# A two-layer graph network: the first layer's vector, tensor and scalar work in hand-set stages, in the order of the source

## The chip, the cores and the metric

The kernel runs on one core of a Trainium2 chip. The metric is the device time of one execution in microseconds; the time before is the median of 11 runs, 1776.19 us (1766.92 to 1780.38).

## The reference

There are 6,250 nodes with 128 features and about 106,000 directed edges (50,000 pairs, both ways, and a loop for each node), sorted by destination. Two layers follow each other, each on a normalized and rectified copy of the node features, and each added to them:

```python
h = jnp.maximum(_layernorm(x), 0.0)
xw = h @ W
out = segment_sum(xw[src] * (dinv[src] * dinv[dst])[:, None], dst) + b   # over the edges and a loop
x = x + relu(out)                                                      # first layer
h = jnp.maximum(_layernorm(x), 0.0)
q, k, v = h[src] @ Wq.T + bq, h[dst] @ Wk.T + bk, h[dst] @ Wv.T + bv   # 8 heads of 16
e = exp(clip(sum(q * k, head) / 4, -10, 10))
out = segment_sum(e / segment_sum(e, src)[src] * v, src) + h
x = x + layernorm(out) * gamma + beta                                  # second layer
```

`dinv` is one over the root of a node's degree. The first layer sums over edges by destination, the second by source, so the kernel also sorts the edges by source while it works on the first layer.

## The kernel before

Nodes are held in 49 blocks of 128; edges, sorted by destination, in 831 tiles of 128, four tiles to a group. A head computes degrees and the table `gtab` of scaled `xw` rows. Then `layer0` runs, and `layer1` after a branch on a flag that `layer0` works out. The change is in `layer0` alone.

`layer0` does three things beside each other.

- **Gathered blocks.** Blocks 16 to 48 are summed by gathering rows. The loop over 142 groups (`GA` to `NG0`) issues four gathers on GpSimd's queue (line 398; five buffers `gt` of four tiles), four matmuls of the gathered rows with a one-hot of the destination into PSUM (`ps`, line 957), and an add of the sum into `acc` at an offset read from memory (`add`, line 939). The one-hot is made three groups ahead (line 928).
- **Counted blocks.** The first 16 blocks (`PC`) need no gather. Windows of edges are fetched (`fetch_windows`, 4 fetches on GpSimd's queue), `count_pair` makes one-hots (`win_oh`, line 772) and `put_counts` multiplies them into counts of edges between nodes (`cb`, line 783, copied by ScalarE into the one tile `counts`, line 786); `product` multiplies a block's counts with the table in three bfloat16 parts, 147 matmuls (line 798).
- **Sorting.** `keys`, 50 sign passes on ScalarE (`counts`, line 537), 25 `rank`s on VectorE (a compare, a scan, a predicated copy, lines 553 to 556), `positions`, then `place` for each of the 831 tiles: one-hots on VectorE (`oh_tau`, line 646; lane tiles `ol`, lines 625 and 627, for eight tiles at a time), a scaled copy on ScalarE (`ola`, line 644), and `put`, six tiles later, matmuls into `pp` (line 659).

A finished block goes through `finish0`, a generator whose parts are run one at a time by `advance`: the own row's add, bias and rectifier, statistics, a normalized copy `hs`, a transpose, the projection to q, k, v (lines 893 and 894), and the split of q (and of k, v for the first 18 blocks) into three bfloat16 parts. Each part ends in writes on SP's queue. PSUM for these chains comes from two banks (`bank`, `let_go`, `free`).

`beside(k)` runs pieces of two lists, `todo` (sorting) and `more` (counted blocks), up to a share that grows with the step k; each piece has a cost that is a weight and no time. In this version these functions only record instructions. The order on each engine is set by the framework's planner, which puts together what it expects to be ready; the source's order is a priority for it. So the source's steps and the order on the chip differ.

Of the kernel before, what the change touches and what calls it, by code (L numbers as in the profile page):

```python
# [19 lines left out]
PE = mybir.EngineType.PE  # L20

P = 128
# [18 lines left out]
CQ = 4  # L41
CR = 8
# [11 lines left out]
class Kernel:  # L54
# [347 lines left out]
    def layer0(self):  # L402
# [19 lines left out]
        with ExitStack() as l0c:  # L422
# [199 lines left out]

            def lanes(t0, n):
                r["ol"] = l0.tile([P, 2, P, PT], F16, name="ol", bufs=2)
                nc.vector.tensor_tensor(r["ol"][:, 0, :, :n], self.lanes[:, :, :n],  # L625
                                        r["lane"][:, None, t0:t0 + n].to_broadcast([P, P, n]), op=OP.is_equal)
                nc.vector.tensor_tensor(r["ol"][:, 1, :, :n], r["ol"][:, 0, :, :n],  # L627
                                        r["b"][:, None, t0:t0 + n].to_broadcast([P, P, n]), op=OP.mult)

            def place(t):  # L630
                lo, hi = window(t)
                on_vector = t // PT % 4 == 3
                if t % PT == 0:
                    n = min(PT, EC - t)
                    lanes(t, n)
                    if on_vector:
                        r["ola"] = l0.tile([P, P, PT], F16, name="ola_v", bufs=1)
                        nc.vector.tensor_tensor(r["ola"][:, :, :n], r["ol"][:, 0, :, :n],
                                                r["a16"][:, None, t:t + n].to_broadcast([P, P, n]), op=OP.mult)
                if on_vector:  # L640
                    ola = r["ola"][:, :, t % PT]
                else:
                    ola = l0.tile([P, P], F16, name="ola", bufs=LAG + 4)
                    nc.scalar.activation(ola, r["ol"][:, 0, :, t % PT], AF.Copy, scale=r["a"][:, t:t + 1])  # L644
                oh = l0.tile([P, CELLS_IN * NB], F16, name="oh_tau", bufs=LAG + 4)
                nc.vector.tensor_scalar(oh[:, :(hi + 1 - lo) * NB], self.slot16[:, lo * NB:(hi + 1) * NB],  # L646
                                        r["code"][:, t:t + 1], None, op0=OP.is_equal)
                placed.append((t, lo, hi, oh, r["ol"], ola))
                if len(placed) > LAG:
                    put()  # L650
# [81 lines left out]
            def fetch_windows(q):  # L732
                rows = l0.tile([P, 2, P], I32, name="win", bufs=2)
                m = CQ * CW
                nc.gpsimd.indirect_dma_start(
                    out=rows[:m].rearrange("p a b -> p (a b)"), out_offset=None, in_=self.wins,
                    in_offset=bass.IndirectOffsetOnAxis(ap=self.win_row[:m, q:q + 1], axis=0))
                ints = l0.tile([P, 2, P], I32, name="win_int", bufs=1)
                nc.vector.tensor_scalar(ints[:m, 0, :], rows[:m, 0, :], 7, None, op0=OP.arith_shift_right)
                nc.vector.tensor_scalar(ints[:m, 1, :], rows[:m, 0, :], P - 1, None, op0=OP.bitwise_and)  # L740

                val = l0.tile([P, 2, P], F32, name="win_val", bufs=1)
                nc.vector.tensor_scalar(val[:m, 0, :], rows[:m, 1, :], self.win_node[:m, q:q + 1], float(NB),
                                        op0=OP.subtract, op1=OP.mult)
                nc.vector.tensor_tensor(val[:m, 0, :], val[:m, 0, :], ints[:m, 0, :], op=OP.add)
                nc.vector.tensor_copy(val[:m, 1, :], ints[:m, 1, :])
                pt, k = bank()
                for i in range(2):
                    nc.tensor.transpose(pt[:, i * P:i * P + m], val[:m, i, :], self.ident[:m, :m])
                code = l0.tile([P, P], F32, name="win_code", bufs=2)  # L750
                nc.scalar.copy(code[:, :m], pt[:, :m])
                lane = l0.tile([P, P], F16, name="win_lane", bufs=2)
                nc.scalar.copy(lane[:, :m], pt[:, P:P + m])
                let_go(k)
                wins[q] = [code, lane]

            counted = []

            def count_pair(b, j):
# [3 lines left out]
                oh = l0.tile([P, 2, 256], F16, name="win_oh", bufs=4)  # L763
# [12 lines left out]
                if len(counted) > 2:  # L776
                    put_counts()

            def put_counts():
                j, oh, ols = counted.pop(0)  # L780
                cb = cbps.tile([P, 512], F32, name="cb")
                for h in range(2):
                    nc.tensor.matmul(cb[:, h * CN * NB:(h + 1) * CN * NB], ols[h], oh[:, h, :CN * NB], start=True,  # L783
                                     stop=True)
# [3 lines left out]
            prods, done = {}, {}  # L788

            def product(b, b0, b1):  # L790
                if b0 == 0:
                    while counted:
                        put_counts()
# [6 lines left out]
                if b1 == NB:  # L800
                    done[b] = prods.pop(b)
                    chains.append(finish0(b, done[b]))
# [3 lines left out]
            todo += [(2, lambda b=b, n=n: counts(b, n), 0) for b, n in groups(NB + 1, 5)] + [(1, offsets, 1)]  # L806
# [9 lines left out]
            more = []  # L816
            for b in range(PC):
                if b % CQ == 0:
                    more.append((0.1 if b else 1.0, lambda q=b // CQ: fetch_windows(q), 1))
                more += [(0.6, lambda b=b, j=j: count_pair(b, j), 0) for j in range(CW // 2)]  # L820
                more += [(1.0, lambda b=b, k=k, n=n: product(b, k, k + n), 0) for k, n in groups(NB, 17)]
# [6 lines left out]
                     [more, lambda k: n2 * (k - 4) / (half - 4), 0.0]]  # L828
            chains = []

            def beside(k):
                for l in lists:
                    while l[0] and l[2] < l[1](k):
                        c, f, wants = l[0][0]
                        if wants and not free() or l[0] is more and done:
                            break
# [3 lines left out]

            def advance():
                for c in chains[:]:
                    if next(c, 0) == 0:
                        chains.remove(c)
# [16 lines left out]
            def finish0(b, po=None):  # L861
                own, xs = loads.pop(b)
                if po is None:
# [5 lines left out]
                    while not free():  # L869
                        yield 1  # L870
                    po, k = bank()
                    nc.tensor.transpose(po[:, :P], mine, self.ident)
                    nc.vector.tensor_add(own, own, po[:, :P])
                    let_go(k)
                else:
                    nc.vector.tensor_add(own, own, po[:, :P])
                    done.pop(b)
                nc.vector.scalar_tensor_tensor(own, own, self.dinv[:, b:b + 1], self.b0_r, op0=OP.mult, op1=OP.add)
                nc.vector.scalar_tensor_tensor(xs[:, 0, :], own, 0.0, xs[:, 0, :], op0=OP.max, op1=OP.add)
                rs, nm = self.stats(fin, xs, 1, self.eps0)  # L880
# [3 lines left out]
                nc.sync.dma_start(xtab_v[:, b, :], xs[:, 0, :])  # L884
                yield 1
                while not free():
                    yield 1
# [9 lines left out]
                kv = qkv[:, D:]  # L897
                nc.sync.dma_start(kvtab_v[:, b, :], kv)
                nc.sync.dma_start(owntab_v[:, b, :], qkv[:, :D])

                qp = fin.tile([P, 3, D], BF16, name="qp")
                q = fin.tile([P, D], F32, name="q")
                nc.scalar.copy(qp[:, 0, :], pw[:, P:2 * P])
                nc.vector.tensor_sub(q, pw[:, P:2 * P], qp[:, 0, :])
                let_go(k)
                if b < PB:
                    kvp = fin.tile([P, 3, 2 * D], BF16, name="kvp", bufs=1)
                    nc.scalar.copy(kvp[:, 0, :], kv)
                    r1 = fin.tile([P, 2 * D], F32, name="r1", bufs=1)
                    nc.vector.tensor_sub(r1, kv, kvp[:, 0, :])  # L910
                yield 1
                nc.scalar.copy(qp[:, 1, :], q)
                if b < PB:
                    nc.scalar.copy(kvp[:, 1, :], r1)
                nc.vector.tensor_sub(qp[:, 2, :], q, qp[:, 1, :])
# [7 lines left out]
            ohs, sums, ats = {}, {}, {}  # L923
# [7 lines left out]
            def add(g):  # L931
# [8 lines left out]
                while blocks and self.done_at[blocks[0]] <= g:  # L940
                    chains.append(finish0(blocks.pop(0)))

            load0(blocks[0])
            for g in range(GA, GA + 3):
                onehot(g)
            for g in range(GA, self.NG0):
                n = size[g]
                gt = self.rows_of_l0.tile([P, G0, D], F32, name="gt")
                for j in range(n):
                    self.gather(gt[:, j, :], self.gtab, idx0, g * G0 + j)  # L950
                if g + 3 < self.NG0:
                    onehot(g + 3)
                beside(g - GA + 1)
                oh = ohs.pop(g)
                ps = sums[g] = l0ps.tile([P, WIN], F32, name="ps")
                for j in range(n):
                    nc.tensor.matmul(ps, gt[:, j, :], oh[:, j, :], start=(j == 0), stop=(j == n - 1))  # L957
                if g > GA:
                    add(g - 1)
                advance()  # L960
            add(self.NG0 - 1)
            while chains:
                advance()
# [641 lines left out]
```

## Time and profile before

| | |
|---|---|
| median of 11 runs | 1776.19 us |
| profiled execution | 1771.92 us |
| its span | 1769.8 us |
| TensorE matmuls busy | 1495.3 us (84%) |
| VectorE busy | 1500.7 us (85%) |
| ScalarE busy | 968.6 us (55%) |
| GpSimd busy | 1169.7 us (66%) |
| mean granted TensorE clock | 0.877 |
| first gather of the first layer | 72.1 us |
| last gather of the first layer | 951.5 us |
| layer 1's first matmul | 996.0 us |

The profile is of one execution; times within it count from the start of its span. "Busy" is the union of an engine's instructions. A matmul's end is modelled, so a busy TensorE need not be at its peak. Register loads and semaphore instructions are not counted as busy. An arrow in a wait names what ended it.

### The profile page before, as it was taken

Reading aid. Unit: us, or ns where it says so; the run is one execution under the profiler, and the core shown is the slowest. Engines: PE = TensorE matmul, PEld = TensorE weight load, DVE = VectorE, ACT = ScalarE, POOL = GpSimd, SP = SyncE. Lnnn points to the kernel's source line nnn. Section 1 sums busy time; section 2 is a strip of 40 time slices with the busy share of each in tenths; the row PEclk is TensorE's granted clock in tenths of the full one; section 3 lists DMA queues with packets and bytes.
Section 4 is the critical chain, followed back from the end, with each engine's and each line's share of the span. In section 5 each row is a group of like instructions: output and inputs, shape, how many; then the busy total and the mean of one; then the engine's idle time right before and its main releaser. Section 6 shows DMA issues by size and latency. Waiting matters only on the chain. (4 is left out here: it accounts for less than half of the span.)

```text
span 1769.8 us, 41293 instructions
## 1 busy us (share of the span) xinstructions
PE 1495.3 (84%) x14772; PEld 1319.9 (75%) x14772; DVE 1500.7 (85%) x4532; ACT 968.6 (55%) x2507; POOL 1169.7 (66%) x1124
## 2 busy tenths in 40 slices
PE   3356788888878889988875499999999999999997
PEld 2346676777667767765663489999999999999997
DVE  8852399998987989999982598998998998998988
ACT  6745544444437788888751244544544544544545
POOL 0377762467567777777774777777677677677660
PEclk9756699999978555699985799999999999999999
DMA  5412232333223222222234975575565655565540
GB/s 118 112 48 58 76 106 78 85 99 101 80 81 104 70 72 73 68 70 67 73 80 151 296 223 176 161 240 174 175 211 170 197 174 175 173 187 157 171 146 25
DMA packets 168378, 225.46 MB, mean 127 GB/s; under 512 B 30187, under 2 KB 127964, under 8 KB 168164
## 3 DMA queue, kind: packets, MB, share of 16 engines
q0 software_dynamic: 45264, 112.89, 23.1%
q1 hardware_dynamic: 116551, 106.65, 19.7%
q10 hardware_dynamic: 6348, 3.20, 0.8%
q8 instruction: 118, 1.93, 0.5%
q14 instruction: 97, 0.79, 0.1%
HBM read 191.42 MB, written 31.20 MB: 126 GB/s over the span
## 5 line engine op out<-in xcount | busy, mean ns | idle before, releaser
L398 POOL DMA_INDIRECT gt<-gtab,idx x567 | 608.8, 1074 | 334.8 <-issue 138.7
L398 POOL DMA_INDIRECT kv<-kvtab,idx x539 | 550.9, 1022 | 193.0 <-issue 125.7
L1041 PE MATMUL pk<-kvp,ohD 128*128 128x256 bf16 x2646 | 314.1, 273 | 5.3 <-ACT kvn L1044 5.3
L644 ACT ACTIVATE ola<-ol,a_f 128x128 f16<-128x128 f16 x624 | 270.4, 524 | 39.0 <-DVE ol L625 35.7
L1041 PEld LDWEIGHTS <-ohD 128*128 128x128 bf16 x2646 | 258.9, 98 | 35.4 <-issue 5.9
L957 PE MATMUL ps<-oh,gt 128*128 128x64 f32 x1134 | 215.7, 334 | 78.0 <-DMA gt<-gtab,idx 31.4
L957 PEld LDWEIGHTS ps<-oh,gt 128*128 128x128 f32 x1134 | 193.4, 246 | 97.0 <-DMA gt<-gtab,idx 36.7
L1049 PE MATMUL pq<-qb,ohT 128*128 128x128 bf16 x2940 | 205.6, 219 | 0.0
L659 PE MATMUL pp<-oh_tau,ol 128*128 128x49 f16 (+5 forms) x916 | 182.5, 258 | 15.4 <-DVE ol L627 12.9
L1067 ACT ACTIVATE ex<-att 128x32 f32<-128x32 f32 x245 | 56.3, 230 | 254.5 <-DVE att L1065 246.3
L1049 PEld LDWEIGHTS <-ohT 128*128 128x128 bf16 x2940 | 185.7, 98 | 5.2
L646 DVE TENSOR_SCALAR oh_tau<-slot,code 128x98 f16<-128x98 f16 (+5 forms) x831 | 172.0, 273 | 3.4 <-PE pp L659 3.4
L786 ACT CAST counts<-cb 128x490 bf16<-128x490 f32 x208 | 112.8, 575 | 108.5 <-PE cb L783 107.6
L798 PEld LDWEIGHTS <-counts 128*128 128x128 bf16 x2352 | 166.3, 153 | 6.9 <-ACT counts L786 6.1
L798 PE MATMUL cb<-xwp,counts 128*128 128x128 bf16 x2352 | 167.1, 239 | 4.1 <-ACT counts L786 4.1
L1063 DVE TENSOR_REDUCE att<-pr 128x32 f32<-128x512 f32 x245 | 165.0, 674 | 0.6
L1055 ACT COPY oh<-ot 128x512 f32<-128x512 f32 x245 | 141.5, 578 | 43.1 <-PE ot L1053 43.0
L659 PE MATMUL pp<-oh_tau,ola 128*128 128x49 f16 (+5 forms) x688 | 143.8, 252 | 19.2 <-ACT ola L644 2.3
L659 PEld LDWEIGHTS <-ol 128*128 128x128 f16 x916 | 128.9, 154 | 25.9 <-DVE ol L627 20.4
L1044 ACT COPY kvn<-pk 128x512 f32<-128x512 f32 x196 | 110.3, 576 | 38.5 <-PE pk L1041 38.0
L659 PEld LDWEIGHTS <-ola 128*128 128x128 f16 x688 | 72.7, 114 | 74.1 <-ACT ola L644 68.5
L783 PE MATMUL cb<-win_oh,win_ol 128*128 128x245 f16 x416 | 86.0, 298 | 48.6 <-DVE win_oh L772 21.7
(1282 smaller groups left out, 2841.4 us busy)
## 6 DMA issues: line engine op xcount, KB each, us to landing
lr<-lrow SPq DMA_DIRECT2D x48, 640.0 KB
dr<-drow SPq DMA_DIRECT2D x48, 288.0 KB
gt<-gtab,idx POOLq DMA_INDIRECT x567
kv<-kvtab,idx POOLq DMA_INDIRECT x539
kvtab<-kvout SPq DMA_DIRECT2D x49, 128.0 KB
kvo<-kvtab SPq DMA_DIRECT2D x5, 1024.0 KB
qtab<-qp SPq DMA_DIRECT2D x49, 96.0 KB
qb<-qtab SPq DMA_DIRECT2D x48, 96.0 KB
```

Source lines behind the costliest of these rows:

```text
L398: self.nc.gpsimd.indirect_dma_start(out=to, out_offset=None, in_=table, in_offset=bass.IndirectOffsetOnAxis(ap=idx[:, t:t + 1], axis=0))
L644: nc.scalar.activation(ola, r["ol"][:, 0, :, t % PT], AF.Copy, scale=r["a"][:, t:t + 1])
L646: nc.vector.tensor_scalar(oh[:, :(hi + 1 - lo) * NB], self.slot16[:, lo * NB:(hi + 1) * NB], r["code"][:, t:t + 1], None, op0=OP.is_equal)
L659: nc.tensor.matmul(pp[:, h, (x0 - f0) * NB:(x1 - f0) * NB], o, oh[:, (x0 - lo) * NB:(x1 - lo) * NB], start=False, stop=t == EC - 1, skip_g ...
L786: nc.scalar.copy(self.counts[:, c0:c0 + 2 * CN, :].rearrange("p n b -> p (n b)"), cb[:, :2 * CN * NB])
L798: nc.tensor.matmul(prods[b][:, :D], self.counts[:, :P, k], self.xwp[:, k, x, :], start=(k, x) == (0, 0), stop=(k, x) == (NB - 1, 2))
L957: nc.tensor.matmul(ps, gt[:, j, :], oh[:, j, :], start=(j == 0), stop=(j == n - 1))
L1041: nc.tensor.matmul(pk[:, i - c, :], ohD[:, h, i * P:(i + 1) * P], kvp[:, 2 * tiles[i] + h, x, :], start=(h, x) == mine[0], stop=(h, x) == ...
L1044: nc.scalar.copy(kv[:, c:c + w, :], pk[:, :w, :])
L1049: nc.tensor.matmul(pq[:, i * D:(i + 1) * D], left, qb[:, x * D:(x + 1) * D], start=(x == 0), stop=(x == 2))
L1055: nc.scalar.copy(oh[:, :n, :], ot[:, :n, :])
L1063: nc.vector.tensor_reduce(att[:, :n * H], pr[:, :n, :].rearrange("p g (h d) -> p (g h) d", h=H), axis=AX.X, op=OP.add)
```

## The change

VectorE, TensorE and ScalarE keep the source's order inside the loop (`tc.manual_schedule`), and the source is set out in stages to suit that. GpSimd's and SP's queues are still ordered by the planner.

- In step g the loop now issues the gathers of group g, then the matmuls of group g - 2, the add of g - 3, the one-hot of g itself, the own-row adds of finished products (`take_products`), one part of each chain (`advance`), and the lists (`beside`).
- `fetch_windows` is split into asking, turning and keeping; the asking is some pairs ahead. A pair's one-hots are multiplied four pairs later (`CP`), not two, and a block's product stands after the first four pairs of the next block, in pieces of 9 and not 17.
- `beside` takes pieces of both lists in turn, and a list that must wait no longer ends the other's turn. `more` starts at step 1 and not 4; the weights change, and sign passes are single pieces.
- Chains keep two stages apart, and `finish0` has more and shorter stages; the split of q reads the copy in SBUF; the write of `xtab` is issued ahead of the statistics.
- The one-hots of pairs and of placing share one set of nine buffers, `wide`, where pairs had four and placing ten.

On each engine the instructions are nearly the same in number and size; their order is not. In the new order the first product (step 6), the first rank (step 26), the position step (61), the first placed tile (67) and the last (129) can be read off the built program.

```diff
+CP = 4
...
+            WIDE = LAG + 3
...
-                oh = l0.tile([P, CELLS_IN * NB], F16, name="oh_tau", bufs=LAG + 4)
+                oh = l0.tile([P, 2, 256], F16, name="wide", bufs=WIDE).rearrange("p a b -> p (a b)")
...
-                oh = l0.tile([P, 2, 256], F16, name="win_oh", bufs=4)
+                oh = l0.tile([P, 2, 256], F16, name="wide", bufs=WIDE)
...
-                if len(counted) > 2:
+                if len(counted) > CP:
...
+            def take_products():
+                while due:
+                    b = due.pop(0)
+                    own = loads[b][0]
+                    nc.vector.tensor_add(own, own, done.pop(b)[:, :P])
+                    chains.append([0, finish0(b)])
...
-            todo += [(2, lambda b=b, n=n: counts(b, n), 0) for b, n in groups(NB + 1, 5)] + [(1, offsets, 1)]
+            todo += [(1.2, lambda b=b: counts(b, 1), 0) for b in range(NB + 1)] + [(1, offsets, 1)]
...
+            def products(b):
+                return [(0.5, lambda k=k, n=n: product(b, k, k + n), 0) for k, n in groups(NB, 9)]
...
             for b in range(PC):
...
+                these = pairs(b)
+                if b:
+                    these[CP:CP] = products(b - 1)
...
+            more += [(0.2, put_counts, 0)] * CP + products(PC - 1)
...
-                     [more, lambda k: n2 * (k - 4) / (half - 4), 0.0]]
+                     [more, lambda k: n2 * (k - 1) / (half - 1), 0.0]]
...
             def advance():
+                before = 99
                 for c in chains[:]:
-                    if next(c, 0) == 0:
-                        chains.remove(c)
+                    if c[0] + 2 <= before:
+                        moved = next(c[1], 0)
+                        if moved == 0:
+                            chains.remove(c)
+                            continue
+                        c[0] += moved == 1
+                    before = c[0]
...
-            for g in range(GA, GA + 3):
-                onehot(g)
-            for g in range(GA, self.NG0):
-                n = size[g]
-                gt = self.rows_of_l0.tile([P, G0, D], F32, name="gt")
-                for j in range(n):
-                    self.gather(gt[:, j, :], self.gtab, idx0, g * G0 + j)
-                if g + 3 < self.NG0:
-                    onehot(g + 3)
-                beside(g - GA + 1)
-                oh = ohs.pop(g)
-                ps = sums[g] = l0ps.tile([P, WIN], F32, name="ps")
-                for j in range(n):
-                    nc.tensor.matmul(ps, gt[:, j, :], oh[:, j, :], start=(j == 0), stop=(j == n - 1))
-                if g > GA:
-                    add(g - 1)
-                advance()
-            add(self.NG0 - 1)
-            while chains:
-                advance()
+            with tc.manual_schedule(engines={DVE, PE, ACT}):
+                for g in range(GA, self.NG0 + 3):
+                    if g < self.NG0:
+                        gt = gts[g] = self.rows_of_l0.tile([P, G0, D], F32, name="gt")
+                        for j in range(size[g]):
+                            self.gather(gt[:, j, :], self.gtab, idx0, g * G0 + j)
+                    if GA <= g - 2 < self.NG0:
+                        gt, oh, n = gts.pop(g - 2), ohs.pop(g - 2), size[g - 2]
+                        ps = sums[g - 2] = l0ps.tile([P, WIN], F32, name="ps")
+                        for j in range(n):
+                            nc.tensor.matmul(ps, gt[:, j, :], oh[:, j, :], start=(j == 0), stop=(j == n - 1))
+                    if GA <= g - 3:
+                        add(g - 3)
+                    if g < self.NG0:
+                        onehot(g)
+                    take_products()
+                    advance()
+                    beside(g - GA + 1)
+                while chains or todo:
+                    advance()
+                    beside(2 * steps)
```

## The prediction

> **What bounds the kernel now.** I read the busy rows in 40 slices (44.2 us each) first, for where no engine is full.
>
> ```profile
> PE   3356788888878889988875499999999999999997
> DVE  8852399998987989999982598998998998998988
> POOL 0377762467567777777774777777677677677660
> PEclk9756699999978555699985799999999999999999
> ```
>
> Layer 1 starts in the 23rd slice and is not touched by the change, so it ends as much earlier or later as the first layer does. Inside the first layer VectorE (DVE) has a hole in slices 4 and 5 (digits 2, 3) and is full later; GpSimd (POOL), which issues the gathers, has its holes where VectorE is full. Engines that take turns in being late are what to look for. So I cut the first layer into stages, first all engines, then POOL's gathers alone (line 398; "x" is their number):
>
> ```profile
> 107.00:225.00 118.00, 82.35 (x549) 67.80 (x550) 42.60 (x176) 65.03 (x137) 89.97 (x93) 0.62 0.25 66
> 225.00:541.00 316.00, 259.20 (x2719) 227.54 (x2719) 287.80 (x891) 144.48 (x370) 175.24 (x164) 0.91 0.32 89
> 560.00:907.00 347.00, 303.42 (x2323) 230.23 (x2324) 329.17 (x1293) 280.48 (x690) 270.27 (x245) 0.77 0.27 72
> ```
>
> ```profile
> 107.00:225.00 118.00, 86.99 (x90) 0.62 0.25 66
> 225.00:541.00 316.00, 175.24 (x164) 0.91 0.32 89
> 560.00:907.00 347.00, 270.27 (x245) 0.77 0.27 72
> 907.00:952.00 45.00, 34.34 (x36) 0.62 0.31 79
> ```
>
> Columns: PE, weight loads, VectorE, ScalarE, POOL, clock, DMA. Until 225 us the gathers run at 118/90 = 1.31 us each, VectorE is 36% busy. From 225 to 541 VectorE is 91% busy and a gather takes 1.93 us. From 560 to 907 (the placing of edge tiles) VectorE is 95% busy and a gather takes 1.42 us. Who holds the gathers in the middle stage is in the waits (us, times, longest), here from 250 to 550 us; the last line is of 550 to 900:
>
> ```profile
> POOL gt L398 <- PE ps L957: 67.2, 9, 20.9
> POOL gt L398 <- PE cb L783: 19.4, 11, 10.3
> ```
>
> ```profile
> POOL gt L398 <- PE pp L659: 14.9, 46, 0.8
> ```
>
> A gather waits up to 20.9 us for the matmul that frees its buffer. Why the middle stage is so full stands in the timeline:
>
> ```profile
> 158.10 11.66 PE L798 MATMUL cb<-xwp,counts 128*128 128x128 bf16 x147
> 206.61 11.38 PE L798 MATMUL cb<-xwp,counts 128*128 128x128 bf16 x147 [0.72 <-ACT counts L786]
> 218.03 0.29 DVE L876 TENSOR_TENSOR own<-own,cb 128x128 f32<-128x128 f32 x1 [8.03 <-PE cb L798]
> 225.04 2.07 DVE L555 TENSOR_TENSOR_SCAN scan<-keep,init,pp 128x896 f32<-128x896 f16 x1
> ```
>
> By 225 us only two of the 16 block products are done, and the first of 25 rank scans starts there. The other 14 products and all ranks are packed into the next 316 us. In the chain that ended last the last gather starts at 951.47 and layer 1's first matmul at 996: those 45 us of drain and loads stay.
>
> ```profile
> 951.47 3.63 DMA gt<-gtab,idx
> 960.63 9.93 DMA htab<-hs
> 989.96 5.92 DMA qb<-qtab
> ```
>
> **The change, part by part.** The profiled execution took 1771.92 us (span 1769.8); the median of the runs is 4.3 us above it. I work out the start of the last gather, 951.5 before, and put the difference on the median. Steps are counted as in the new loop, one step for each of the 142 groups of four gathers. What an instruction occupies is taken start to start from runs of the same kind in the trace.
>
> *Until step 25.* The fetch of the windows stands behind 20 gathers on POOL's queue, as before, so the first window values come at 108 us in both. Three of the four fetches now stand together there; the third needs the first one's buffer, which VectorE reads at 108: 1 us at most. From step 2 on the new order makes a product about every four steps: five are done by step 25. VectorE has 79 us of work in steps 2 to 25, which is no bound. POOL alone would allow step 25 (it needs 88 gathers) at 108 + 68 x 1.31 = 197, about 200 us. TensorE decides: in four steps one product (147 matmuls at 134.49/1911 = 0.070, or 23.03/294 = 0.078 in the slow clock: 10.3 to 11.5 us), 26 matmuls of count pairs (0.12 at full clock, 0.20 in the mean of 225 to 541: 3.1 to 5.2), four groups of gather matmuls (45.60 us for 318 rows of eight a group: 1.15; in the slow clock 1.97: 4.6 to 7.9), a chain's transposes and projection (1.5). That is 19.5 to 26.1 us, 4.9 to 6.5 a step. I take 5.1, near the fast end, because the long product itself is where the clock rose in the trace. Step 25 then stands at 108 + 23 x 5.1 = 225 us; bounds 200 and 258. So the first rank comes when it came before, but with five products behind it and not two.
>
> The Trainium skill (TensorE: Matmul & The Clock Gate, "What's actually happening") says the half clock is the default and one busy window of about 3.4 us lifts it. By its half clock for everything the four steps would take 26 us, my slow bound; the trace agrees that it lifts inside a product, and that from 107 to 225 the mean grant was 0.62.
>
> *Steps 26 to 61*, the ranks, are VectorE's: 25 ranks of 0.95 + 1.99 + 1.11 = 4.05 us (101), 230 one-hots of 0.205 (47), 29 lane tiles of 0.61 (18), 36 times a group's one-hot and add, 0.34 + 0.13 (17), 18 chains of 1.6 (29), the position step (18), five reads of the accumulator offsets (1.7 each, 8), two window turns (3): 241 us. In the old middle stage VectorE, those reads included, was filled to about 94%. With a fixed order I take 93%: 259 us; bounds 97% and 88%, 248 and 274. TensorE's 4.9 a step is below VectorE's 6.7. Here POOL falls behind VectorE's pace and waits on its five buffers; that costs nothing more.
>
> *Steps 62 to 66* have 12 us of VectorE work but the last two products on TensorE, waited for by the own-row add at the next step: 2 x 10.5 + 5 x 1.15 + 1.5 = 28 us (25 to 31).
>
> *Placing*, steps 67 to 129. The same instructions in nearly the same order as before: 803 tiles took 347 us with their chains and groups, 0.432 each; 831 make 359. The one-hots now share nine buffers and not ten; a little more, 362. Bounds 350 (the 351 us of VectorE work without a gap) and 385.
>
> *The end.* Old placing ended at 907 with 36 gathers to go in 44 us. At step 130 POOL can be four groups ahead, 32 gathers at 1.25: 40 us. Chains now keep two stages apart, which costs two or three stages of about 1.5 us after the last gather: 4 us (0 to 8).
>
> Sum: 225 + 259 + 28 + 362 + 40 = 914, with 4 for the end 918, against 951.5: 33.5 us less. 1776.2 - 33.5 = 1743. With all bounds at their good ends 200 + 248 + 25 + 350 + 40 = 863 (-88); at their bad ends 258 + 274 + 31 + 385 + 44 + 8 = 1000 (+48). Not all meet; my own range for this case is -65 to -5.
>
> Things with one answer: the read of q from SBUF where PSUM was read, the table write moved ahead of the statistics, the written-out statistics: same engines, same sizes, nothing on the path. Earlier release of a PSUM bank helps a chain that is now staged anyway. SP's transfers keep the planner's order: a write that waits holds up loads for later blocks behind it. Before, one write held SP for 86.4 us, and VectorE's own-row adds waited for TensorE alone (35.6 us), never for their load; I cost it at nothing, and at one load's few us a chain if that cover goes.
>
> One more price is POOL's own. Where VectorE is idle an issue takes 0.97 us (98 to 225 us), where it is 95% busy 1.11. If the whole layer ran at the 1.42 us spacing of placing, 547 gathers after 108 us would end at 885: below my 914, so it is no bound yet, but little below. The Trainium skill (SBUF — State Buffer, "A bandwidth-pool intuition" and the box ahead of it on DMAs issued by GpSimd) speaks against filling VectorE: its two-port modes lock GpSimd out while it writes descriptors. By its example (620 ns alone, about 3100 beside VectorE, a factor of five) 547 gathers would take an estimated 2,800 us; the trace shows 14% on the issue.
>
> **The rivals.** *Gathers become the bound early* (faster still): step 25 at 200 us and ranks at 97%: 25 + 11 us on top of the forecast, -70, 1707. For it: the 67.2 us wait goes away. Against: TensorE's 0.62 clock in that stage.
>
> *Placing loses its slack* (slower). TensorE, in fixed order, now does a group's four matmuls in one piece (1.04 to 1.97 us) and a chain's projection (1.59 + 0.53 in the slow clock) ahead of the tiles; VectorE's one-hots can be six tiles ahead in a queue of nine, so three tiles, 1.3 us, are all that hides it. Before, the group's matmuls stood two by two between tiles, and VectorE waited only 6 us here for TensorE. The price is 0.2 us a step if only steps with a projection show it, 1.4 if each does; 0.9 over 63 steps is 57 us: 914 turns into 971, 1776 + 23 = 1799. It decides from 33.5/63 = 0.53 us a step.
>
> *TensorE stays at the half clock* through the first stage and VectorE waits for products: 258 and 274 in the sum, 48 us more than forecast: 966 against 951.5, 1791. For it: the 0.62 of that stage. Against: 0.91 in the next, where TensorE is 82% busy, as it would be here. Where two thirds of it hold, there is no difference.
>
> **How the numbers follow.** Forecast 0.50, gathers early 0.20, placing 0.20, half clock 0.10. A measurement of this kernel tells 0.2%, 3.6 us, from no change. Faster: 0.50 (less 0.02) + 0.20 + 0.03 = 0.71; same 0.04; slower 0.25. The range leaves out the lowest third of the second case and the upper half of the slower ones: 1703 to 1792; the likeliest case alone is 1711 to 1771.
>
> **What would show it.** Right: VectorE's digits in slices 4 and 5 rise to 5 or more; five products before the first scan; no gather waits over 10 us; the first scan near 225 us, first placed tile near 512, last gather near 914. Wrong: step 25 later than 258 us, or a placing stage over 385 us with VectorE waiting for TensorE on the shared one-hot buffers, or layer 1 longer than its 774 us.

## The result, and the profile after

The changed kernel takes **1884.51 us** (median of 8 runs, 1880.44 to 1887.24), where before takes 1775.84 (31 runs): a ratio of 1.0613, interval 1.0597 to 1.0629. It is 108.7 us slower, where 33 us less were forecast. The profiled execution took 1883.37 us, its span 1880.8. Layer 1 takes 772.9 us (773.4 before), so all of it lies in the first layer: its last gather starts at 1062.4 us and not at 951.5.

The busy rows of the changed kernel, a slice being 47.0 us:

```profile
PE   4367678776875788888887649999999999999997
DVE  8753349877866689999998349899899998998988
POOL 0365355545553567777767477777767767677670
PEclk9666778677676655678998569999999999999999
```

VectorE's hole in slices 4 and 5 is still there (3, 3; 5 or more was forecast), and a second one has opened in slices 12 to 14 (6, 6, 6). The granted clock, at 9 in slices 6 to 11 before, is 6 to 8 there now. The same stages, cut where first rank and placing now begin (columns as before: PE, weight loads, VectorE, ScalarE, POOL, clock, DMA), and then POOL's gathers alone:

```profile
107.00:290.00 183.00, 137.36 (x1145) 119.52 (x1145) 81.83 (x333) 108.30 (x239) 94.98 (x96) 0.69 0.23 64
290.00:571.00 281.00, 208.79 (x1882) 181.79 (x1880) 223.46 (x578) 95.71 (x234) 149.62 (x138) 0.73 0.26 73
635.00:1012.00 377.00, 313.88 (x2398) 244.83 (x2397) 356.23 (x1348) 297.30 (x726) 271.79 (x252) 0.74 0.26 70
```

```profile
107.00:290.00 183.00, 93.78 (x94) 0.69 0.23 64
...
1012.00:1062.00 50.00, 37.09 (x39) 0.62 0.33 88
```

Until the first rank a gather now takes 183/94 = 1.95 us, not 1.31. In the middle stage VectorE is busy 80% (223 of 281), not 91%, and the clock is 0.73, not 0.91. Only placing is as full as it was (356 of 377, 94%). The gathers' waits, of 285 to 640 us and then of 635 to 1012:

```profile
POOL gt L400 <- PE ps L1008: 78.2, 15, 12.0
...
POOL gt L400 <- PE cb L796: 16.5, 10, 4.1
```

```profile
POOL gt L400 <- PE pp L664: 27.6, 38, 3.8
```

The waits for the matmul that frees a buffer have not gone: the longest is 12.0 us where it was 20.9, but there are 15 of them where there were 9. What stands there now is in the timeline: two products, the add that takes the second, and the first rank's scan.

```profile
153.52 10.96 PE L809 MATMUL cb<-xwp,counts 128*128 128x128 bf16 x147
...
184.11 11.02 PE L809 MATMUL cb<-xwp,counts 128*128 128x128 bf16 x147
...
195.16 0.29 DVE L821 TENSOR_TENSOR own<-own,cb 128x128 f32<-128x128 f32 x1 [11.96 <-PE cb L809]
...
290.33 2.08 DVE L557 TENSOR_TENSOR_SCAN scan<-keep,init,pp 128x896 f32<-128x896 f16 x1
```

VectorE stands still for 11.96 us, the whole of the product, with nothing that may pass the add. The chain that ended last has kept its tail (1107.9 - 1062.4 = 45.5 us from the last gather to layer 1, 45 before):

```profile
1062.36 3.38 DMA gt<-gtab,idx
...
1071.14 9.74 DMA qtab<-qp
...
1101.04 6.41 DMA qb<-qtab
```

### The profile page after: what moved, and what is told of

Same layout as the page of the kernel before. It is cut to its first block, busy times and chain, and to the rows that moved or that the text cites. A ratio compares the mean times of both kernels' runs of the same rounds, so it can differ in the third digit from the quotient of the medians.

```text
span 1880.8 us, 41151 instructions
## 1 busy us (share of the span) xinstructions
PE 1534.0 (82%) x14772; PEld 1360.0 (72%) x14772; DVE 1532.9 (82%) x4532; ACT 977.8 (52%) x2507; POOL 1163.3 (62%) x1124
## 5 line engine op out<-in xcount | busy, mean ns | idle before, releaser
L1008 PE MATMUL ps<-oh,gt 128*128 128x64 f32 x1134 | 210.4, 347 | 11.4 <-DMA gt<-gtab,idx 6.3
L1008 PEld LDWEIGHTS ps<-oh,gt 128*128 128x128 f32 x1134 | 201.4, 265 | 14.5 <-DMA gt<-gtab,idx 7.8
L664 PE MATMUL pp<-wide,ol 128*128 128x49 f16 (+5 forms) x916 | 183.4, 261 | 34.3 <-DVE wide L651 33.8
L809 PEld LDWEIGHTS <-counts 128*128 128x128 bf16 x2352 | 178.3, 154 | 21.1 <-ACT counts L799 18.6
L809 PE MATMUL cb<-xwp,counts 128*128 128x128 bf16 x2352 | 179.8, 248 | 13.7 <-ACT counts L799 13.7
L796 PE MATMUL cb<-wide,win_ol 128*128 128x245 f16 x416 | 97.6, 356 | 102.0 <-ACT counts L799 63.3
L664 PE MATMUL pp<-wide,ola 128*128 128x49 f16 (+5 forms) x688 | 147.4, 258 | 28.9 <-ACT ola L649 12.4
L651 DVE TENSOR_SCALAR wide<-slot,code 128x98 f16<-128x98 f16 (+5 forms) x831 | 160.6, 277 | 5.1 <-PE pp L664 4.9
L796 PEld LDWEIGHTS <-win_ol 128*128 128x128 f16 x416 | 59.3, 159 | 129.5 <-issue 82.4
```

Source lines behind the costliest of these rows:

```text
L664: nc.tensor.matmul(pp[:, h, (x0 - f0) * NB:(x1 - f0) * NB], o, oh[:, (x0 - lo) * NB:(x1 - lo) * NB], start=False, stop=t == EC - 1, skip_g ...
L809: nc.tensor.matmul(prods[b][:, :D], self.counts[:, :P, k], self.xwp[:, k, x, :], start=(k, x) == (0, 0), stop=(k, x) == (NB - 1, 2))
```

## The experiments

The change has two halves: the new stages, and the order held on three engines. Theory A says that the held order costs the time, theory B the stages. Further theories say which engine and by what; they are named as they came up; A1, A2 and A3 put the cost on ScalarE, TensorE and VectorE.

e1 to e8, e13 to e16 and e18 ran on chips where every kernel is slower: before takes 2216 to 2270 us there, layer 1 some 1060 to 1110. Those runs are compared only by their ratio to before on the same chip and among themselves. e9 to e12 and e17 ran on chips like that of the first measurement (before at 1772 to 1776).

### Which held order costs the time

All of these are the changed kernel with another set of engines in one line; e1, e6 and e10 hold none.

```diff
-            with tc.manual_schedule(engines={DVE, PE, ACT}):
+            if True:                                          # e1, e6, e10
+            with tc.manual_schedule(engines={DVE, PE}):       # e2, e16, e18
+            with tc.manual_schedule(engines={DVE, ACT}):      # e3, e15
+            with tc.manual_schedule(engines={PE, ACT}):       # e4, e11
+            with tc.manual_schedule(engines={PE}):            # e13, e17
+            with tc.manual_schedule(engines={ACT}):           # e14
```

**e1 to e4.**

> The changed source with its stages, but no engine held to the source's order: the planner orders all five. Theory A (the loss comes from holding engines to the source's order): the product and the count pairs overlap again, the stage up to the first rank scan shortens from 290 to about 230 us, and the time falls to 1750 to 1800. Theory B (the stages themselves, lags of two and three groups and products cut in and put between pairs, cost it): about 1884 as in the changed kernel, at least 1850.

> VectorE and TensorE held to the source's order, ScalarE not. Theory A1 (ScalarE's fixed order is the cause: a sign pass of 1.2 us stands between every two count copies, so TensorE waits for its PSUM buffer): a pair takes 0.6 and not 1.5 us, five products come 8 us a product earlier, first scan at about 240 us and not 290, time 1830 to 1845. Theory A2 (TensorE's fixed order is: a product of 11 to 14 us in one piece, with VectorE's next step waiting for it): no change, 1875 to 1890.

> VectorE and ScalarE held, TensorE not. Theory A2: VectorE's waits for products (78 us) and for gather matmuls (78 us) go mostly, time below 1820. Theory A1: only the part that is not ScalarE's, time 1860 to 1885.

> TensorE and ScalarE held, VectorE not. VectorE can then go past a wait for a product to the one-hots of later pairs and to ranks. Theory A3 (VectorE's fixed order is the cause, as it alone stands still for 12 us at an own-row add): time below 1820. Theories A1 and A2: 1860 to 1885, since a free VectorE runs ahead only as far as the nine one-hot buffers let it.

Measured, as ratios to before (2270.48): e1 0.989 (0.985 to 0.993), e2 0.998 (0.993 to 1.003), e3 1.013 (1.004 to 1.022), e4 0.989 (0.984 to 0.993). The numbers expected belong to the other chips, and none of the four was as slow as 1.06. So the changed kernel itself was needed as a yardstick.

**A yardstick (e5, e6).**

> The changed kernel itself, as the yardstick for the others on the same chip. All theories: about 1884 us where the kernel before takes 1776 (ratio 1.06), first layer's last gather near 1062, signs done near 283, step 25 near 286.

> The new stages, but no engine held to the source's order (on a chip where e5 is the yardstick). Theory A (the held order costs it): 1750 to 1790 us, 95 to 130 less than e5. Theory B (the stages and their order of recording cost it, the planner cannot mend that): 1850 to 1885. Theory P (a count pair waits on TensorE for a copy that stands behind a sign pass on ScalarE, which a planner may reorder): 1790 to 1830, signs done before 260.

e5, the changed kernel: 2294.97 us, ratio 1.012 (1.005 to 1.019), not 1.06. e6: 2249.51, 0.993 (0.988 to 0.998). On these chips the held order costs 45 us, and most of the loss is not there. In their profile TensorE has idle time that nothing in the profile explains ("issue"), and the mean granted clock is lower in layer 1 too (0.88 from 1200 to 1900 us of e5, 1.00 from 1120 to 1820 of the changed kernel's first profile). Here are waits of e5 in layer 1 (1200 to 1900 us), which the change does not touch:

```profile
PEld L1096 <- issue: 88.0, 117, 2.1
...
PE pk L1096 <- issue: 57.2, 101, 2.3
```

In the first profile of the changed kernel matmuls have no such wait there, and the weight loads of that line 5.9 us over the whole run. What makes it was not found.

**e9 to e11.**

> The kernel before, unchanged, profiled on the chip of this call. It tells two readings of the runs so far apart, in which layer 1 took about 1105 us and not 773 on the chips of two calls. If the chip's slowness stretches every stage alike, the first layer of before takes 879 x 1.08 = 950 us there (the changed kernel's went from 990 to 1067), and its middle stage about 340. If it stretches above all the stages in which the engines are full, the first layer takes 1020 to 1060. On a chip where layer 1 takes 773 all agree: 1776, first layer 879.

> The new stages, no engine held to the source's order, as in e1 and e6. Where layer 1 takes 773 us: theory A (the held order costs the 108 us) 1760 to 1790; theory B (the stages cost it) 1860 to 1890. If the loss of 29 us and the gain of 45 measured on the other chips scale with nothing, 1830 to 1845, half and half. Where layer 1 takes 1105 us: ratio 0.99 as before.

> The changed kernel with VectorE alone free of the held order, TensorE and ScalarE held. Theory A3 (VectorE stands at adds for TensorE's products and gather matmuls, with other work behind them): nearly all of e10's gain over the changed kernel, within 15 us of e10. Theory A2 (TensorE's held order: count pairs wait there for ScalarE's copies) or A1 (ScalarE's): at most a third of e10's gain.

e9 took 1770.76 us with a first layer (first to last gather) of 877.6: the chip is like the first ones, and e9's question of the slower chips stays open. e10, the stages with no engine held, takes **1726.29 us**, ratio 0.973 (0.962 to 0.983), 46 us less than before (1772.02) and 158 less than the changed kernel, which was measured on another chip; by the two ratios it is 157. Theory B falls; theory A holds with a larger sum than it was given. e10 is the fastest version of this study. e11, VectorE free and the other two held, takes 1835.05, 1.034 (1.022 to 1.046): 49 us, a third of the 158, come with VectorE's order on top of the other two. That is what A1 and A2 said and far from A3.

**e13 to e18.**

> TensorE alone held to the source's order. Numbers for a chip on which before takes 1772 to 1776, none held 1726, TensorE and ScalarE held 1835, all three 1884. Theory T (TensorE's held order is the price): 1800 to 1835. Theory S (ScalarE's held order is): 1726 to 1750. Theory TS (only the two together, since a free ScalarE would copy counts in time): 1726 to 1760, and e14 as low.

> ScalarE alone held. Theory T: 1726 to 1745. Theory S: 1790 to 1835, with the sign passes done near 283 as in the changed kernel and not near 206 as with none held. Theory TS: 1726 to 1760.

> VectorE and ScalarE held, TensorE free. Theory T: 1740 to 1785, TensorE's free order takes away most of 158 us. Theory S: 1850 to 1885. Theory TS: 1750 to 1800. VectorE's own share, 49 us by e11, would remain in the first and last case: 1775.

> VectorE and TensorE held, ScalarE free. Theory T: 1850 to 1885. Theory S: 1740 to 1785, signs done near 206. Theory TS: 1775 to 1800.

> TensorE alone held, again, for a chip where before takes 1772 to 1776. Theory S (ScalarE's held order is the price, as e13 and e14 say of their chip): 1705 to 1745, as fast as none held (1726) or faster. Theory T (TensorE's): 1800 to 1835, clock in the first stage near 0.7 as in e11. In between, 1745 to 1800, both share it. On a chip like e13's: ratio 0.98 to 0.99.

> The changed kernel with ScalarE alone free of the held order (VectorE and TensorE held, as in e2 and e16), for a chip where before takes 1772 to 1776. If each engine has its own price: 1758 + 49 = 1807, signs done near 206. If ScalarE's price needs TensorE held (count pairs) but VectorE's needs ScalarE held: 1758 to 1775. If VectorE's order alone would already make TensorE wait as ScalarE's does: 1850 to 1885. On a chip like e2's: ratio 0.99 to 1.01.

Ratios to before, all sets together:

| held | slower chips | chips as at first |
|---|---|---|
| none | 0.989 (e1), 0.993 (e6) | 0.973 (e10), 1726 us |
| TensorE | 0.983 (0.972 to 0.994) (e13) | 0.990 (0.986 to 0.994) (e17), 1758 us |
| ScalarE | 1.025 (1.014 to 1.037) (e14) | not run |
| TensorE, ScalarE | 0.989 (e4) | 1.034 (e11), 1835 us |
| VectorE, ScalarE | 1.013 (e3), 1.020 (1.007 to 1.033) (e15) | not run |
| VectorE, TensorE | 0.998 (e2), 1.005 (1.000 to 1.009) (e18) | not run |
| all three | 1.012 (e5) | 1.061, 1884 us |

e16 repeats e2 (2219.72 us beside 2215.64) and has no interval. On the chips as at first, adding one engine after the other costs 32 us for TensorE, 77 for ScalarE on top of it, 49 for VectorE on top of both. These shares hold for this order of adding: on the slower chips ScalarE alone held has the highest ratio of all, and with TensorE held beside it the loss is gone (0.989), so an engine has no price of its own. e17 lies between theory S (1705 to 1745) and T (1800 to 1835), in the band set down for "both share it", nearer S. On the slower chips TensorE alone held is faster than before, and not told apart from none held. In e14 the sign passes end only at 401 us, where theory S expected 283. Whether 77 us would come back if ScalarE alone were freed is open: e18 was to tell and met a slower chip, where 1.005 stands beside e5's 1.012, with intervals that overlap.

### Where the waits are

From 107 us to the end of the last product the same work is done in each kernel (3,410 to 3,450 matmul records). Two of the rows, for the changed kernel and for e10:

```profile
107.00:634.00 527.00, 387.76 (x3421) 337.93 (x3420) 340.27 (x1011) 219.32 (x509) 270.24 (x258) 0.71 0.25 68
```

```profile
107.00:500.00 393.00, 337.09 (x3413) 295.00 (x3414) 327.45 (x1050) 216.72 (x511) 281.66 (x262) 0.88 0.32 92
```

| held | stretch, us | TensorE busy | TensorE idle | clock |
|---|---|---|---|---|
| before | 448 | 354 | 94 | 0.83 |
| none (e10) | 393 | 337 | 56 | 0.88 |
| TensorE (e17) | 417 | 350 | 67 | 0.83 |
| TensorE, ScalarE (e11) | 474 | 381 | 93 | 0.75 |
| all three | 527 | 388 | 139 | 0.71 |

VectorE's busy time hardly moves (327 to 340). Of the 134 us between e10 and the changed kernel 83 are idle time of TensorE, and 51 the same matmuls under a lower clock. Who makes TensorE idle, and who waits for TensorE, is in the waits (us, times, longest) of e17, e11 and the changed kernel over these stretches:

```profile
ACT kvout L948 <- PE ps_f L946: 70.3, 18, 8.5
...
DVE acc L992 <- PE ps L1008: 26.6, 14, 7.2
PE cb L796 <- ACT counts L799: 26.0, 61, 1.6
DVE own L821 <- PE cb L809: 25.7, 6, 6.3
ACT rs L929 <- DVE bn_mv L927: 24.5, 12, 9.4
```

```profile
ACT kvout L948 <- PE ps_f L946: 108.2, 21, 10.6
...
PE cb L796 <- ACT counts L799: 64.0, 64, 4.6
...
DVE acc L992 <- PE ps L1008: 54.4, 30, 10.4
...
ACT rs L929 <- DVE bn_mv L927: 44.0, 15, 12.1
...
PE cb L796 <- DVE wide L784: 1.4, 3, 0.9
```

```profile
ACT kvout L948 <- PE ps_f L946: 103.9, 21, 10.9
...
DVE own L821 <- PE cb L809: 78.5, 14, 12.0
PE cb L796 <- ACT counts L799: 63.3, 55, 3.0
...
DVE acc L992 <- PE ps L1008: 59.3, 15, 11.6
...
PE cb L796 <- DVE wide L784: 34.9, 15, 7.0
```

With ScalarE held (from the first fence to the second) TensorE waits 64 us for count copies where it waited 26; e10 has 17.7. With VectorE held too (third fence) its own-row adds wait 78.5 us where they waited 25. ScalarE stands longest at `kvout`, a projection that on TensorE lies behind a product; a copy behind it can't pass.

The third fence also shows how VectorE's order reaches TensorE. The one-hots of later pairs stand on VectorE behind the adds that wait for products, so TensorE in turn waits 34.9 us for one-hots (`wide`) where it waited 1.4 in e11; that is 33.5 of the 46 us of idle time that VectorE's order adds. This wait follows the setting in all runs with the new stages, over the same stretch of each: 27 to 50 us in eight of the nine with VectorE held (85 in e8, which is told below), 0.5 to 11.4 in the nine with VectorE free, on both kinds of chips.

The count copies can be followed one by one. The time from a pair's end on TensorE to the start of its copy adds up to 56 us in e10, 45 in e17, 134 in e11 and 142 in the changed kernel. In that time ScalarE was inside a sign pass for 13, 7, 47 and 48 us, and stood idle ahead of the square root of a chain's statistics (line 929, waiting for VectorE) for at most 2, 4, 36 and 27 us. In the order of the source 35 or 36 of the 50 sign passes stand right before a count copy; the planner leaves 9 to 11 there. But the last sign pass ends at 283 us, and 32 of TensorE's 63 us of waits for copies come after it (28 of 64 in e11), so sign passes can explain about half of that wait at most. The changed kernel:

```profile
204.07 0.55 ACT L799 CAST counts<-cb 128x490 bf16<-128x490 f32 x1
204.51 1.04 ACT L539 ACTIVATE junk<-blk,bias 128x896 f16<-128x896 f16 x1
204.67 0.57 PE L796 MATMUL cb<-wide,win_ol 128*128 128x245 f16 x2 [1.40 <-ACT counts L799]
...
205.55 0.56 ACT L799 CAST counts<-cb 128x490 bf16<-128x490 f32 x1
206.00 1.05 ACT L539 ACTIVATE junk<-blk,bias 128x896 f16<-128x896 f16 x1
206.16 0.57 PE L796 MATMUL cb<-wide,win_ol 128*128 128x245 f16 x2 [0.92 <-ACT counts L799]
```

Here a pair takes 1.49 us (204.67 to 206.16), of which TensorE works 0.57. In e10 sign passes run together while a product is on TensorE, and then copies run end to end:

```profile
208.33 2.20 ACT L799 CAST counts<-cb 128x490 bf16<-128x490 f32 x4 [0.42 <-PE cb L796]
...
208.52 0.79 PE L796 MATMUL cb<-wide,win_ol 128*128 128x245 f16 x4
```

Four copies, one for each pair, take 2.20 us: a pair in 0.55.

### Is it the sign passes, or the pairs' buffers?

**e7 and e12** put the sign passes back to five at a time, so that all are recorded by step 14; e7 in the changed kernel, e12 in e11. **e8** puts a block's waiting pairs ahead of its product, as before did.

```diff
-            todo += [(1.2, lambda b=b: counts(b, 1), 0) for b in range(NB + 1)] + [(1, offsets, 1)]
+            todo += [(2, lambda b=b, n=n: counts(b, n), 0) for b, n in groups(NB + 1, 5)] + [(1, offsets, 1)]   # e7, e12
...
-CP = 4
+CP = 2                                          # e8
...
                 if b0 == 0:
+                    while counted:              # e8
+                        put_counts()
...
-                if b:
-                    these[CP:CP] = products(b - 1)
...
-                more += these
+                more += these + products(b)     # e8
...
-            more += [(0.2, put_counts, 0)] * CP + products(PC - 1)
```

> The changed kernel, but the sign passes go back to five at a time at weight 2, as in the kernel before: all are recorded by step 14 rather than 26, and the first rank there. Order still held. Theory P (sign passes between the count copies): the sign passes leave the stretch with the products, step 25 comes 15 to 30 us earlier than in e5 or the ranks end 15 to 50 us earlier, time 1835 to 1870. Theory A (any held order loses the same): 1880 to 1890. Theory Q (one of two count buffers is held by a product in pieces, so pairs go one at a time): 1875 to 1890.

> As e11, with the sign passes back at five together and weight 2, so that all are recorded by step 14 and the first rank there. If work for a free VectorE was missing early (it is 45% busy until the first rank), this beats e11 by 20 to 50 us and may come below the kernel before by as much. If what bounds the stretch until placing is TensorE with its products and pairs, it equals e11 within 10 us, as e7 equalled e5.

> The changed kernel, but a block's waiting count pairs are all put before its product, as in the kernel before, and two pairs wait rather than four; the product still comes in six pieces. Order still held. Theory Q: pairs then have both count buffers except behind a product; 13 pairs a block at 0.6 to 0.9 us instead of 1.5, up to 8 us for each of 16 blocks: 1780 to 1850. Theory P: the copy behind a sign pass is still waited for, 1870 to 1890. Theory A: 1870 to 1890. A loss (1890 to 1930) if the five pairs waiting hid VectorE's one-hots.

e7: signs end at 206 us (e5: 297) and the first scan comes at 225 (305), but the last at 579 (596), placing starts at 676 (671), and the time is 2298.57 beside e5's 2294.97: no gain. e12, on the other kind of chip: 1844.39, ratio 1.039 (1.029 to 1.050), 9 us behind e11 and within its interval. Only 7 sign passes stand before a copy, but in clumps of five, and the pairs' copies are as late as before (148 us in sum, 61 of them inside sign passes). So moving sign passes in a held queue is no cure; a run without them was not made. Later work doesn't follow a first rank that comes 74 us earlier (211 in e12, 285 in e11): theory P falls as a full explanation, and the other explanation of e12's expectation, that TensorE with its products and pairs bounds the stretch, fits. e8: 2330.37, 1.028 (1.020 to 1.036), 35 us worse than e5, so the gain of theory Q did not come. Its trace says why the time rose: TensorE waits 28.2 us for copies where it waited 41.2 in e5, but 85.0 us for one-hots where it waited 35.2. That is the loss that the expectation named: the pairs held back had covered VectorE's one-hots.

What the runs show is that the held order costs the 158 us, and that TensorE's wait for one-hots comes with VectorE's order. That the waits for copies behind ScalarE's other work make the 77 us of ScalarE is read from the traces, and no run that removes these waits alone was made. On the slower chips freeing ScalarE alone leaves TensorE 20 to 25 us of waits for copies (e2, e16, e18) where e5 has 41, and 43 to 50 us for one-hots.

## Why the prediction was wrong

The parts of the sum, in us:

| part | forecast | changed | e10, none held | e17, TensorE |
|---|---|---|---|---|
| to the first rank | 225 | 290 | 236 | 241 |
| first rank to first placed tile | 287 | 345 | 252 | 270 |
| placing | 362 | 377 | 369 | 369 |
| last placed tile to last gather | 44 with the end's 4 | 50 | 51 | 57 |
| last gather | 918 | 1062 | 909 | 937 |

**The failed step is "TensorE decides" until step 25, and the 93% that follows it.** The forecast summed what instructions occupy, and left out what the change added beside them: a queue that may not pass a waiting instruction. With no engine held the total comes within 17 us (1726 measured, 1743 forecast). That is partly luck: the parts of e10 are off by +11, -35, +7 and +7 us, and cancel.

*Until step 25.* Four steps were to take 19.5 to 26.1 us, and 4 x 5.1 = 20.4 was put; from step 6 to 26 they took 4 x (286.4 - 120.4)/20 = 33.2. In 107 to 290 us a product takes 11 to 12 us (10.3 to 11.5 forecast), four groups 4 x 37.2/24 = 6.2 (4.6 to 7.9), a chain's projection and transpose 16.4/7 = 2.3 (1.5). The 26 pair matmuls take (37.6 busy + 35.4 idle)/156 = 0.47 each, 12.2 us where 3.1 to 5.2 were put: this is the term that was mis-sized. 31.3 of the 35.4 us of idle time are waits for count copies. The forecast's upper price of a pair's matmul, 0.20 us, was busy time alone, and the forecast named no wait of TensorE for ScalarE. The kernel before had this wait, though a small one (107 to 555 us):

```profile
PE cb L783 <- ACT counts L786: 13.7, 34, 1.1
```

In e10 a pair's matmuls take (30.6 + 12.4)/156 = 0.28 each, 7.2 us for 26, so the term was too small even without a held order. The slow bound was too low as well: 26.1 us was called the half clock for everything, but its 0.078 us for a product's matmul is a mean of a stretch granted 0.62, in which the first matmuls of each product are 0.107 us apart and the later ones 0.064. That five products stand ahead of the first rank was right, and earned nothing.

*Steps 26 to 66.* The work was right: VectorE is busy 249 us from 286 to 595 (steps 26 to 61; 241 forecast). But 93% was put and 81% measured, 309 us for 259. In this stretch its own-row adds wait 29.4 us for products and its adds of a group's sum 19.7 us for their matmuls. The forecast had priced the wait "by the own-row add at the next step" for the last two products alone, 28 us; from 595 to the first placed tile at 635 it took 40. Over the whole stretch with the 16 products that add waits 14 times, 78.5 us in all.

*Placing and the end* were right within 15 and 6 us. **The rival that placing loses its slack** asked for more than 0.53 us a step; the wait of VectorE's one-hots for `pp` there is 4.9 us in all, 0.08 a step. **The half clock** pointed at the right rows: 0.69 and 0.73 were granted, and the prediction's own argument against it, that TensorE would be 82% busy, failed since TensorE was 75 and 74% busy there. But its price of 48 us covers only part of the 144 between 918 and 1062. **Gathers early** did not come: it asked for step 25 at 200 us, and already before the first rank gathers wait up to 11.9 us for a gather matmul's buffer (24.7 in seven waits).

## What to carry to other kernels

When a change holds an engine to the source's order, the sum of what its instructions occupy is a floor: list for each engine the instructions that wait for another engine, and price what is queued behind each of them. Look first at short instructions on which another engine depends: here a count copy, which frees a small PSUM buffer, and a pair's one-hots. When they stand behind a long or waiting instruction, the engine that needs them waits too. Moving one kind of such instructions (the sign passes) earned nothing while other waiting ones stayed ahead of the copies. A better arrangement of the source and a held order are two changes, and are worth measuring apart: here the first gains 46 us and the second loses 158.

## What was not expected of the hardware

The granted clock goes with the time that TensorE stands in pauses, most of them short. From 107 us to the last product:

| held | pauses over 0.5 us | their sum, us | over 3.4 us | mean clock |
|---|---|---|---|---|
| none (e10) | 31 | 37 | 2 | 0.88 |
| TensorE (e17) | 40 | 47 | 1 | 0.83 |
| before | 63 | 75 | 1 | 0.83 |
| TensorE, ScalarE (e11) | 57 | 82 | 2 | 0.75 |
| the same, sign passes five at a time (e12) | 42 | 95 | 10 | 0.73 |
| all three | 70 | 132 | 4 | 0.71 |

The Trainium skill (TensorE: Matmul & The Clock Gate, "HAM oscillation — how this bites in real kernels") gives as the rule that no pause should exceed about 3.4 us. Two pauses in e10 and four in the changed kernel do, so that rule does not tell the two apart. In these six stretches the clock nowhere rises as the sum of the pauses grows, and the number of pauses, short or long, does not order it. That is a relation over six rows, and no run here changed the pauses alone.

On some chips every kernel here takes about 2250 us, before and after alike, and the held order costs 2% there instead of 9. TensorE's waits without a visible cause (88.0 and 57.2 us above) and a lower granted clock go with it. Why TensorE and ScalarE held together beat before there (0.989) and lose to it elsewhere (1.034) stays open.
